# Chunk ends of the first pass in three parts, set-up transposes a block later, more of layer 1 left for the tail

## The chip, the cores and the metric

The kernel runs on one core of a Trainium2 chip. The metric is the device time of one execution in microseconds (us). The core's engines run side by side, each in its own order: PE does matrix products (and transposes, as products with the identity), DVE (VectorE) and ACT (ScalarE) do elementwise work, POOL (GpSimd) small elementwise work and part of the DMA issues, SP (SyncE) the other DMA issues. They meet at semaphores.

## The reference

Two layers over N = 4096 nodes with 512 features each; `adj` is a 0/1 matrix of 4096 x 4096.

```python
# layer 0, H = 8 heads of FH = 64
feats = einsum('nf,hfo->hno', X, W)
dense = s_self[:, :, None] + s_neigh[:, None, :]     # feats . a_self, feats . a_neigh
dense = where(dense > 0, dense, 0.2 * dense) * A
out   = einsum('hij,hjo->hio', softmax(dense), feats) + b
x     = layernorm(x + relu(out))
# layer 1, 32 graphs of 128 nodes each
a      = where(mask, query @ key.T * scale, 0.0)     # mask: same graph
scores = (a + adj + adj) * where(mask, 1.0, -1e6)
x      = layernorm(x + (softmax(scores) * mask) @ value)
```

In layer 0 a pair without an edge has the score 0 and still counts in the softmax with weight 1. So a row of layer 0 is a sum over its neighbours, plus the sum of all features, minus the neighbours' plain features, over a matching denominator.

## The kernel before, in words

The function `adjacency_streamed_path` does the work. (A general path, chosen by a flag, is not run with these inputs.) It has a set-up, four passes over the adjacency matrix and a tail.

**Order.** `tc.manual_schedule(engines={mybir.EngineType.PE})` (L455) makes PE run in program order: the order in which the Python code issues matmuls is PE's order. The orders of DVE, ACT, POOL and SP are chosen by a scheduler when the kernel is built. Tiles come from pools with a fixed number of buffers (`bufs`); an instruction that fills a tile waits until the last reader of the tile that had the buffer before is done.

**Set-up (L578 to L794).** Eight blocks k of four row tiles u (128 nodes each). A block turns the rows of x (L635), makes the features of each tile (`features`, four products that the trace records as four matmuls each for u, L715), the scores (`scores`, L644), their exponentials (`exponentials`, L658 on PE, the rest on ACT and DVE), and the rows of exponentials: `rows_of_exponentials` transposes on PE (L694), copies the result to `pu_row` on ACT (L698) and stores it to DRAM (L702). `columns_of_exponentials` transposes `pu_row` back on PE (L707) and copies it to `pu_all` on DVE (L708). `scaled_features` scales a tile on DVE and ACT (L729, L737, L738) into staging tiles `gst` and `fst` (two buffers each) and stores them to DRAM (POOL, L750), from where the passes read them as `g_s` and `f_s`. At the end PE makes the sum of all features (L785, `S_col`).

**A pass (`main_pass`, L1264).** There are four passes r, each for two heads. A pass has four chunks c of 1024 rows i; a chunk goes over 32 tiles j of 128 neighbours, in cycles of eight tiles (pass 3: four). For a cycle SP loads `f_s` and `g_s`, and from pass 1 on the adjacency tiles `at`. DVE makes `q` (L1311), the weights before the neighbour's own factor, and ACT (some on DVE, L1316) makes `mark` (L1320), which tells the branch of the leaky step. PE's part of a cycle is:

- `accf` (L1331, 32 matmuls in a cycle of eight): plain features of the neighbours;
- in pass 0 the transposes that bring the coming adjacency tiles (`bring`, L1086; ACT casts them, L1090, and POOL stores them for the later passes, L1091);
- `acc` (L1348, 128): the weighted features;
- `dens` (L1362, 32): the denominators; in pass 0 also `ae` (L1375, 16): sums of exponentials and counts of neighbours, for all heads.

In each cycle there are two places for other work, `pieces(c, group, 0)` between `accf` and `acc`, and `pieces(c, group, 1)` behind `acc`. In passes 0 to 2 `run_pieces` fills one of them: it adds a credit of 0.75 times the cycle's width (6.0 for eight tiles) and takes steps from generators until the credit is used; each `yield` says what the step before it cost. There are two queues of generators, `ends` (the ends of chunks) and `work` (weights of layer 1, L862 on; kinds of graphs); before, they are served in turns. In pass 3 the string plan `PLAN` says which generator takes a step in which place: `E` the end of a chunk, `a` and `b` a step of the first and of the second block of layer 1 of the chunk that `E` ended, `R` the layer-0 rows of its second block, and `p` (L1214) a step of what is left of the second block of the chunk before it.

**A chunk's end (`sums_to_rows`, L1125).** Right away, `ys` takes `accf` and `acc` (DVE, L1133 and L1141), and ACT copies `dens` to `dcs` and, in pass 0, `ae` to `aes` (L1143, L1146). PSUM tiles `acc`, `accf` and `dens` have one buffer each, so the next chunk's matmuls wait for these reads. The rest is the generator `pieces`, which first yields a cycle:

- in pass 0, `pz`: eight products of `aes` with `comb` (L1154); DVE makes `n0` and `z_all` of it;
- `pd`: four transposes of `dcs` (L1173); DVE makes `parts` (L1176) and from it `rd`, one over the denominators (L1186 to L1189);
- `fin`: eight transposes of `ys` in two banks (L1196), which DVE scales by `rd` into `hst` (L1197, one buffer); `hst` goes to DRAM as `hs_d` (POOL, L1209), or in pass 3, with the other passes' parts read back as `hp_l`, into the rows of layer 0 (`rows_of_layer_0`, L1121) and on to the two generators of layer 1 for this chunk.

Scratch PSUM banks for all these are handed out in turn by `misc`: two in pass 0, three later.

**Layer 1 (`layer_1`, L929 on)** takes a block of 512 rows in steps: two of transposing its rows (x1T, L935), two of zT (L955, eight matmuls each), one of scores with exponentials (L982; DVE L991, ACT L1016 on), then V, pT, V (L1027, L1056), po (L1041) with layernorm, V and po again, whose rows go to `out`. Behind the passes a last string (`run_plan("bEpppaa...")`) does what is left: the tail.

Of the kernel before, what the change touches and what calls it, by code (L numbers as in the profile page):

```python
# [19 lines left out]
P = 128  # L20
# [384 lines left out]
def adjacency_streamed_path(  # L405
# [172 lines left out]
    with tc.tile_pool(name="setup1", bufs=1, side="right") as one, tc.tile_pool(  # L578
# [174 lines left out]
        for k in range(NB):  # L753
            if k + 1 < NB:
                load_rows(k + 1)
            fbs = [features(k, 0)]
            if k == 0:
                fbs.append(features(k, 1))
                scores(0)
            else:  # L760
                exponentials(k)
            if k + 1 < NB:
                turn_rows(k + 1)
            if k == 0:
                exponentials(0)
            scaled_features(k, 0, fbs[0])
            if k:
                fbs.append(features(k, 1))
            scaled_features(k, 1, fbs[1])
            fbs.append(features(k, 2))  # L770
            scaled_features(k, 2, fbs[2])
            if k + 1 < NB:
                scores(k + 1)
            rows_of_exponentials(k)
            fbs.append(features(k, 3))
            scaled_features(k, 3, fbs[3])
            columns_of_exponentials(k)
            if k in (4, 5, 6):
                tc.keep_in_program_order(load_adjacency(0, 4 * (k - 4)))
        xsum = one.tile([P, FC], F32, name="xsum")  # L780
# [2 lines left out]
        for r in range(PR):  # L783
# [8 lines left out]
        nc.vector.scalar_tensor_tensor(  # L792
            S_col, b_col, float(N), pS, op0=OP.mult, op1=OP.add
        )  # L794

    psa = ctx.enter_context(tc.tile_pool(name="ps_acc_f", bufs=1, space=PSUM))
    dens = psa.tile([P, HB], F32, name="dens")
# [6 lines left out]
    def kind_of_scores(lp):  # L804
        ok = lp.tile([P, 5], F32, name="ok")
        ext = lp.tile([P, 5], F32, name="ext")
        for i, (v, op) in enumerate(
            ((p_all, OP.max), (d_all, OP.max), (p_all, OP.min), (d_all, OP.min))
        ):
            rows = lp.tile([P, NT], F32, name="rows")  # L810
            nc.vector.tensor_reduce(rows, v, AX.X, op)
            nc.vector.tensor_reduce(ext[:, i : i + 1], rows, AX.X, op)
        nc.vector.tensor_reduce(ext[:, 4:5], n0, AX.X, OP.min)
        nc.vector.tensor_scalar(ok[:, 0:2], ext[:, 0:2], P_MAX, None, op0=OP.is_le)
        nc.vector.tensor_scalar(ok[:, 2:4], ext[:, 2:4], 1.0 / P_MAX, None, op0=OP.is_ge)
        nc.vector.tensor_scalar(ok[:, 4:5], ext[:, 4:5], N / 2.0, None, op0=OP.is_ge)
        nc.vector.tensor_reduce(okp, ok, AX.X, OP.add)

    def kind_of_graphs(lp):

# [304 lines left out]
    def sums_to_rows(r, c, acc, accf, ae, u_row, later_by):  # L1125

        its = slice(c * CT, (c + 1) * CT)
        pair = slice(2 * r, 2 * r + 2)  # L1130

        y = evp.tile([P, C], F32, name="ys")
        nc.vector.scalar_tensor_tensor(  # L1133
            y,
            accf.rearrange("p s n -> p (s n)"),
            S_col[:, r : r + 1],
            u_row,
            op0=OP.add,
            op1=OP.mult,
        )  # L1140
        nc.vector.tensor_add(y, y, acc.rearrange("p s n -> p (s n)"))  # L1141
        dcs = evp.tile([P, HB], F32, name="dcs")
        nc.scalar.copy(dcs, dens)  # L1143
        if r == 0:
            aes = pools["aes"].tile([P, HB], F32, name="aes")
            nc.scalar.copy(aes, ae)  # L1146

        def pieces():
            if r < PR - 1:
                yield later_by  # L1150
            if r == 0:
                pz = misc([P, CT, H + 1])
                for t in range(CT):
                    nc.tensor.matmul(  # L1154
                        pz[:, t, :],
                        aes[:, ts(t % 4, P)],
                        comb[:, t // 4, :],
                        start=(t == 0),
                        stop=True,
                        skip_group_check=True,  # L1160
                    )
                nc.vector.tensor_scalar(
                    n0[:, its], pz[:, :, H], -1.0, float(N), op0=OP.mult, op1=OP.add
                )
                z = z_all[:, its, :]
                nc.vector.tensor_tensor(
                    z, u_all[:, its, :], n0[:, its, None].to_broadcast([P, CT, H]), OP.mult
                )
                nc.vector.tensor_tensor(z, pz[:, :, :H], z, OP.add)
                yield 1.5  # L1170
            pd = misc([P, 4, P])
            for t in range(4):
                nc.tensor.transpose(pd[:, t, :], dcs[:, ts(t, P)], ident)  # L1173
            parts = small.tile([P, 2, 4, 2, 2], F32, name="parts")
            for s in range(2):
                nc.vector.tensor_reduce(  # L1176
                    parts[:, s],
                    pd[:, :, 64 * s : 64 * s + 64]
                    .rearrange("p t (h m) -> p t h m", h=2)[:, :, :, :6]
                    .rearrange("p t h (k i) -> p t h k i", k=2),  # L1180
                    AX.X,
                    OP.add,
                )
            parts = parts.rearrange("p s t h k -> p (s t) h k")
            rd = small.tile([P, CT, 2], F32, name="rd2")
            nc.vector.tensor_tensor(rd, parts[:, :, :, 1], p_all[:, its, pair], OP.mult)  # L1186
            nc.vector.tensor_tensor(rd, parts[:, :, :, 0], rd, OP.add)
            nc.vector.tensor_tensor(rd, rd, z_all[:, its, pair], OP.add)
            nc.vector.reciprocal(rd, rd)  # L1189
            if r == 0:  # L1190
                yield 0.6
            hst = hp_.tile([P, CT, FP], F32, name="hst")
            for t4 in range(0, CT, 4):
                fin = misc([P, 4, FP])
                for t in range(4):
                    nc.tensor.transpose(fin[:, t, :], y[:, ts(t4 + t, P)], ident)  # L1196
                nc.vector.tensor_tensor(  # L1197
                    hst[:, t4 : t4 + 4, :].rearrange("p t (h o) -> p t h o", h=2),
                    fin.rearrange("p t (h o) -> p t h o", h=2),
                    rd[:, t4 : t4 + 4, :, None].to_broadcast([P, 4, 2, FH]),  # L1200
                    OP.mult,
                )
                if t4 == 0:
                    if r == PR - 1:
                        first = rows_of_layer_0(2 * c, hst, pools["lp"])
                    if r == 0:
                        yield 0.6
            if r < PR - 1:
                nc.gpsimd.dma_start(  # L1209
                    hs_d[ts(c, C), ts(r, FP)].rearrange("(t p) n -> p t n", p=P), hst  # L1210
                )
            else:
                args = pools["lp"], pools["lp1"], pools["lp2"]
                plan["p"] = plan["b"]  # L1214
                plan["a"] = layer_1(2 * c, first, *args)

                def second():
                    rows = rows_of_layer_0(2 * c + 1, hst, pools["lp"])
                    plan["b"] = layer_1(2 * c + 1, rows, *args)
                    yield  # L1220

                plan["R"] = second()
            yield 1.8

        return pieces()
# [4 lines left out]

    PLAN = ("Ep", ""), ("pp", ""), ("p", "a"), ("Ra", "a"), ("a", "b"), ("ba", "b"), ("ab", ""), (
        "aaba",
        "",
    )
    plan = {"p": None, "b": None}

    def run_plan(todo):
        for k in todo:  # L1240
# [3 lines left out]
            if k == "E":  # L1244
                ends.pop(0)

    state = {"credit": 0.0, "worked": True}

    def run_pieces(budget):

        state["credit"] += budget
        while state["credit"] > 0.0 and (work or ends):
            queue = ends if ends and (state["worked"] or not work) else work
            state["worked"] = queue is work
            try:
                state["credit"] -= next(queue[0])
            except StopIteration:
# [6 lines left out]
    def main_pass(r, ae=None, wide=4):  # L1264

        for c in range(NCH):
# [9 lines left out]
                )  # L1276
            def pieces(c, group, place):
                if r == PR - 1 and c:
                    run_plan(PLAN[group][place])
                elif place == (r == 0):  # L1280
                    run_pieces(0.75 * wide)

# [115 lines left out]
    at2 = wide_passes.enter_context(tc.tile_pool(name="more_at", bufs=MORE))  # L1398
    q2 = wide_passes.enter_context(tc.tile_pool(name="more_q", bufs=2))
    more["at"], more["q"] = (at2, MORE), (q2, 2)  # L1400
    with tc.tile_pool(name="ps_ae", bufs=1, space=PSUM) as psx, tc.tile_pool(
        name="aes", bufs=1
    ) as pools["aes"]:
        ae = psx.tile([P, HB], F32, name="ae")
        nc.vector.memset(ae, 0.0)
        banks.append(psx)
        main_pass(0, ae, wide=8)
        run_pieces(999.0)
        banks.remove(psx)
    first_pass.close()  # L1410
    banks.extend([ctx.enter_context(tc.tile_pool(name="ps_misc2", bufs=2, space=PSUM))] * 2)
# [2 lines left out]
    with tc.tile_pool(name="wl1", bufs=1, side="right") as wp:  # L1414
        work.append(weights_of_layer_1(keep, wp))
        work.append(kind_of_graphs(wp))
        kind_of_scores(wp)
        main_pass(1, wide=8)
        for gen in work:
            for _ in gen:  # L1420
# [5 lines left out]
    with tc.tile_pool(name="lp", bufs=2) as lp, tc.tile_pool(  # L1426
# [2 lines left out]
        pools.update(lp=lp, lp1=lp1, lp2=lp2)  # L1429
        main_pass(3)  # L1430
        plan["K"] = kind_of_inputs(lp1)
        run_plan("bEpppaaRaaKKbbababaababbbb")


@with_exitstack
# [50 lines left out]
```

## Time and profile before

| | us |
|---|---|
| median of four runs (2119.07 to 2122.23) | 2121.45 |
| the profiled execution's own time | 2116.37 |
| its span in the profile | 2114.0 |
| PE busy (97% of the span) | 2059.8 |
| DVE busy (79%) | 1660.2 |
| ACT busy (73%) | 1540.2 |
| a cycle of eight tiles in pass 0 / one with a chunk's end | 25.79 / 32.15 |
| a cycle of eight tiles in pass 1 | 23.13 |

The profile is one execution, which took some 5 us less than the median. Its span runs from the first to the last recorded instruction. Busy time is the sum of an engine's instructions; idle time of PE is put down to what released the instruction that ended it. A row `PE ps_m L1154 <- ACT aes L1146` is time in which PE's instruction at line 1154, writing tile `ps_m`, waited for ACT's instruction at line 1146. Ends of matmuls are modelled, so a longer duration of the same group of matmuls means that it was issued more slowly.

### The profile page before, as it was taken

How to read it: one execution, taken by the hardware profiler on the slowest of the kernel's cores; microseconds unless marked ns; L12 is line 12 of the kernel's file. 1: busy time of each engine (PE TensorE's matmuls, PEld its weight loads, DVE VectorE, ACT ScalarE, POOL GpSimd, SP SyncE). 2: the span in 40 equal slices, each digit the busy share in tenths (PEclk: the TensorE clock that was granted, in tenths of full speed). 3: DMA queues.
4: the chain of work that ended last, by engine and by line, in shares of the span. 5: the costliest groups of instructions: out<-in, count | busy, mean ns of one | idle time of the engine just before them, and what ended most of it. 6: DMA issues, size and time to landing. Idle time of an engine off the chain costs nothing. (4 is left out here: it accounts for less than half of the span.)

```text
span 2114.0 us, 38159 instructions
## 1 busy us (share of the span) xinstructions
PE 2059.8 (97%) x15012; PEld 1019.2 (48%) x15012; DVE 1660.2 (79%) x2032; ACT 1540.2 (73%) x1820; POOL 247.0 (12%) x391
## 2 busy tenths in 40 slices
PE   8999999999999999999999999999999999999987
PEld 4445554555554444545444544444454444445443
DVE  5547887878779978799999999999975884886554
ACT  3327997978859888798899889998875576567420
POOL 2333222222200000000000000000300110110110
PEclk9999999999999999999999999999999999999999
DMA  7889999999988998799999999989974673675211
GB/s 244 265 219 232 288 283 273 275 269 261 291 285 311 325 324 298 265 315 328 334 326 348 307 328 342 327 286 363 308 240 143 228 252 133 229 263 165 70 48 42
DMA packets 207882, 551.29 MB, mean 261 GB/s; under 512 B 25292, under 2 KB 66252, under 8 KB 207692
## 3 DMA queue, kind: packets, MB, share of 16 engines
q1 hardware_dynamic: 140748, 425.79, 58.2%
q0 software_dynamic: 62784, 121.91, 23.0%
q8 instruction: 120, 1.97, 0.4%
q10 hardware_dynamic: 4160, 1.05, 0.2%
q14 instruction: 70, 0.57, 0.1%
HBM read 491.79 MB, written 107.22 MB: 283 GB/s over the span
## 5 line engine op out<-in xcount | busy, mean ns | idle before, releaser
L1311 DVE SCALAR_TENSOR_TENSOR q<-p_row,d_all,at 128x1024 f32<-128x1024 f32 x1024 | 1241.3, 1279 | 177.2 <-PE acc L1348 141.0
L1320 ACT ACTIVATE mark<-q,nb_all 128x1024 fp8e4<-128x1024 f32 x896 | 996.9, 1145 | 205.3 <-DVE q L1311 179.0
L1348 PE MATMUL acc<-q,g_s 128*32 128x512 f32 x8192 | 903.5, 593 | 3.7 <-DVE q L1311 3.2
L1348 PEld LDWEIGHTS acc<-q,g_s 128*32 128x32 f32 x8192 | 264.1, 110 | 598.6 <-issue 536.5
L1331 PE MATMUL accf<-at,f_s 128*128 128x512 f32 x2048 | 493.2, 397 | 1.9 <-issue 1.9
L1331 PEld LDWEIGHTS accf<-at,f_s 128*128 128x128 f32 x2048 | 380.2, 189 | 110.5 <-issue 29.1
L1105 ACT ACTIVATE ck<-ck,neg_half_f 128x1024 f32<-128x1024 f32 x128 | 145.9, 1140 | 19.8 <-DMA ck<-in_adj_dram 19.6
L1106 ACT ACTIVATE ck<-ck,neg_quarter 128x1024 f32<-128x1024 f32 x128 | 146.3, 1143 | 1.8
L1090 ACT CAST at<-ps_m 128x1024 fp32r<-128x1024 fp8e4 x128 | 120.2, 1025 | 14.5 <-issue 10.3
L1362 PE MATMUL dens<-mark,e_b 128*6 128x512 fp8e4 x2048 | 126.3, 384 | 0.0
L715 PE MATMUL ps_set<-w_sb_f,xT_f 128*128 128x512 f32 x256 | 118.8, 614 | 0.0
L1027 PE MATMUL ps_m<-wvT,x1T 128*128 128x512 f32 x256 | 114.3, 594 | 4.1 <-DVE parts L1176 4.0
L955 PE MATMUL ps_m<-x1T,M_sb 128*128 128x512 f32 x256 | 113.0, 595 | 1.2 <-ACT x1T L936 1.2
L1209 POOL DMA_DIRECT2D hs_d<-hst x12 | 10.8, 897 | 843.4 <-DVE hst L1197 744.3
L1316 DVE TENSOR_SCALAR mark<-q,d_all 128x1024 fp8e4<-128x1024 f32 x128 | 95.9, 749 | 5.1 <-DVE q L1311 0.5
L1362 PEld LDWEIGHTS <-e_b 128*6 128x6 bf16 x2048 | 54.3, 87 | 83.4 <-issue 41.9
L1091 POOL DMA_DIRECT2D at_d<-at x128 | 69.1, 540 | 167.3 <-ACT at L1090 91.7
L737 ACT ACTIVATE fst<-fb 128x512 fp32r<-128x512 f32 x32 | 20.3, 636 | 87.3 <-DMA f_d<-fst 53.1
L955 PEld LDWEIGHTS ps_m<-x1T,M_sb 128*128 128x128 f32 x256 | 48.0, 190 | 62.8 <-issue 59.1
L1027 PEld LDWEIGHTS ps_m<-wvT,x1T 128*128 128x128 f32 x256 | 47.7, 190 | 60.1 <-issue 57.7
L715 PEld LDWEIGHTS ps_set<-w_sb_f,xT_f 128*128 128x128 f32 x256 | 49.8, 202 | 51.4 <-issue 51.0
L1035 DVE TENSOR_TENSOR v_t<-ps_m,bv_row 128x512 f32<-128x512 f32 x32 | 21.8, 681 | 63.0 <-PE ps_m L1027 63.0
(172 smaller groups left out, 1142.0 us busy)
## 6 DMA issues: line engine op xcount, KB each, us to landing
at<-at_d SPq DMA_DIRECT2D x384, 512.0 KB, 6.0
ck<-in_adj_dram SPq DMA_DIRECT2D x128, 512.0 KB, 5.2
f_s<-f_d SPq DMA_DIRECT2D x128, 512.0 KB, 7.5
at_d<-at POOLq DMA_DIRECT2D x128, 512.0 KB, 14.7
g_s<-g_d SPq DMA_DIRECT2D x128, 256.0 KB, 5.5
f_d<-fst POOLq DMA_DIRECT2D x32, 512.0 KB, 6.1
p_row<-pu_d SPq DMA_DIRECT2D x32, 512.0 KB, 6.6
a_b<-in_adj_dram POOLq DMA_DIRECT2D x32, 512.0 KB, 17.0
```

The costliest lines, as they stand in the source:

```text
L715: nc.tensor.matmul(pf, tile_j(xTs[k][:, c].rearrange("p u n -> p (u n)"), u), w_sb[:, c, :], start=(c == 0), stop=(c == FC - 1),)
L955: nc.tensor.matmul(pz, L1["M"][:, f, ts(c, P)], x1T[:, f, :], start=(f == 0), stop=(f == FC - 1),)
L1027: nc.tensor.matmul(pv, x1T[:, f, ts(u, P)], L1["wvT"][:, f, :], start=(f == 0), stop=(f == FC - 1),)
L1090: nc.scalar.copy(at, both[:, :, k])
L1105: tc.keep_in_program_order(nc.scalar.activation(ck, ck, AF.Square, bias=neg_half))
L1106: nc.scalar.activation(ck, ck, AF.Abs, bias=neg_quarter, accum_out=binp[:, k : k + 1])
L1311: nc.vector.scalar_tensor_tensor(q, p_row[h], d_j, ats[r, c, j].bitcast(F32), op0=OP.max, op1=OP.mult)
L1316: nc.vector.tensor_scalar(mark, q, d_j, None, op0=OP.is_gt, saturate=False)
L1320: nc.scalar.activation(mark, q, AF.Sigmoid, bias=nb_all[:, j, hh : hh + 1], scale=BIG, saturate=False,)
L1331: nc.tensor.matmul(accf[:, s, :], f_s[j // 4][:, j % 4, w, :], ats[r, c, j][:, ts(s, HB)], start=(j == 0 and w == 0), stop=(j == NT - 1 an ...
L1348: nc.tensor.matmul(acc[o : o + 32, s, :], g_s[j // 4][:, j % 4, h, o % FH : o % FH + 32], qs[j, h][:, ts(s, HB)], start=(j == 0), stop=(j ...
L1362: nc.tensor.matmul(dens[lo : lo + 6, :], e_b[:, j, 2 * r + h, :], marks[j, h][:, ts(s, HB)], start=(j == 0), stop=(j == NT - 1),)
```

## The change

It has these parts:

1. **Set-up.** `columns_of_exponentials(k)` (L707) is issued a block later, behind `features(k + 1, 1)`; the last one behind `S_col`.
2. **Ends of pass 0.** The generator yields a whole cycle (`later_by`) after `pz` and after `pd`, and nothing between the two halves of `fin`. So `pz`, `pd` and `fin` run in the second, third and fourth cycle of the next chunk; before, they ran one after the other in the second.
3. **The last end of pass 0.** `run_pieces(999.0)` behind pass 0 is gone; this end runs in the second to fourth cycle of pass 1, and three scratch banks serve it there.
4. **`aes`** has no buffer of its own; it takes the one buffer of `hst`.
5. **Queues.** `run_pieces` serves `ends` first, then `work`; layer 1's weights come about a chunk later in pass 1, and `kind_of_scores` becomes a generator in `work`.
6. **Pass 3.** The first group of a chunk is `bE` for `Ep`: the other block's V, pT, V comes ahead of `pd` and `fin`. The last chunk has a plan of its own for its last two groups, without two steps of block `b` (one zT step and the scores), and these run in the tail, around the last chunk's end.

```diff
             scaled_features(k, 0, fbs[0])
             if k:
                 fbs.append(features(k, 1))
+                columns_of_exponentials(k - 1)
             scaled_features(k, 1, fbs[1])
...
             fbs.append(features(k, 3))
             scaled_features(k, 3, fbs[3])
-            columns_of_exponentials(k)
...
             S_col, b_col, float(N), pS, op0=OP.mult, op1=OP.add
         )
+        columns_of_exponentials(NB - 1)
...
         nc.vector.tensor_reduce(okp, ok, AX.X, OP.add)
+        yield 0.0
...
         if r == 0:
-            aes = pools["aes"].tile([P, HB], F32, name="aes")
+            aes = hp_.tile([P, CT, FP], F32, name="hst")
+            aes = aes.rearrange("p t n -> p (t n)")[:, :HB]
             nc.scalar.copy(aes, ae)
...
                 nc.vector.tensor_tensor(z, pz[:, :, :H], z, OP.add)
-                yield 1.5
+                yield later_by
             pd = misc([P, 4, P])
...
             nc.vector.reciprocal(rd, rd)
             if r == 0:
-                yield 0.6
+                yield later_by
             hst = hp_.tile([P, CT, FP], F32, name="hst")
...
                         first = rows_of_layer_0(2 * c, hst, pools["lp"])
-                    if r == 0:
-                        yield 0.6
...
-                plan["p"] = plan["b"]
                 plan["a"] = layer_1(2 * c, first, *args)
...
-    PLAN = ("Ep", ""), ("pp", ""), ("p", "a"), ("Ra", "a"), ("a", "b"), ("ba", "b"), ("ab", ""), (
-        "aaba",
-        "",
-    )
-    plan = {"p": None, "b": None}
+    PLAN = [("bE", ""), ("bb", ""), ("b", "a"), ("Ra", "a"), ("a", "b"), ("ba", "b")]
+    PLANS = PLAN + [("ab", ""), ("aaba", "")], PLAN + [("a", ""), ("aa", "a")]
+    plan = {"b": None}
...
-            queue = ends if ends and (state["worked"] or not work) else work
-            state["worked"] = queue is work
+            queue = ends or work
...
                 if r == PR - 1 and c:
-                    run_plan(PLAN[group][place])
+                    run_plan(PLANS[c == NCH - 1][group][place])
...
-    with tc.tile_pool(name="ps_ae", bufs=1, space=PSUM) as psx, tc.tile_pool(
-        name="aes", bufs=1
-    ) as pools["aes"]:
+    with tc.tile_pool(name="ps_ae", bufs=1, space=PSUM) as psx:
...
         main_pass(0, ae, wide=8)
-        run_pieces(999.0)
         banks.remove(psx)
...
-        kind_of_scores(wp)
+        work.append(kind_of_scores(wp))
...
-        run_plan("bEpppaaRaaKKbbababaababbbb")
+        run_plan("bEbbbbbaaRaaKKbbababaababbbb")
```

More of the change, by code (lines that the diff above doesn't have):

```diff
@@ L1245, in run_plan @@
                 ends.pop(0)
-    state = {"credit": 0.0, "worked": True}
+    state = {"credit": 0.0}
     def run_pieces(budget):
```

## The prediction

> **What bounds the kernel now.** I read the busy shares first, then the waits of TensorE (PE), then PE's timeline at each place that the diff touches.
>
> ```profile
> PE 2059.8 (97%) x15012; PEld 1019.2 (48%) x15012; DVE 1660.2 (79%) x2032; ACT 1540.2 (73%) x1820; POOL 247.0 (12%) x391
> ```
>
> PE is the bound, and its order is written by hand. The span is 2114.0 us, so about 54 us are idle; some 12 of these are the output chain at the very end. No PE instruction is removed, so a gain can only be idle time, or matmuls that ran slowly after idle time. In the view of PE's waits (total us, times, longest) I look for those that the edits touch:
>
> ```profile
> PE ps_set L707 <- ACT pu_row L698: 6.4, 3, 3.5
> PE ps_m L1027 <- DVE parts L1176: 4.0, 2, 2.0
> PE ps_m L1154 <- ACT aes L1146: 3.4, 1, 3.4
> PE ps_m L1196 <- DVE rd L1186: 2.3, 3, 0.8
> ```
>
> L707 is the set-up transpose, L1154/L1196 the first pass's chunk ends, L1027 the last pass's chunk boundaries. The timelines (start us, duration us, instruction, idle before) show what each wait drags along. Set-up, PE then ScalarE (ACT):
>
> ```profile
> 66.96 3.60 PE L715 MATMUL ps_set<-w_sb_f,xT_f 128*128 128x512 f32 x8
> 73.06 0.41 PE L707 MATMUL ps_set<-ident_f,pu_row 16*128 16x16 f32 x4 [2.50 <-ACT pu_row L698]
> 73.41 5.41 PE L715 MATMUL ps_set<-w_sb_f,xT_f 128*128 128x512 f32 x8
> ```
> ```profile
> 71.40 0.63 ACT L737 ACTIVATE fst<-fb 128x512 fp32r<-128x512 f32 x1 [7.80 <-DMA f_d<-fst]
> 72.40 0.60 ACT L698 COPY pu_row<-ps_set 16x512 f32<-16x512 f32 x1
> ```
>
> The eight L715 after the wait take 5.41 us instead of 3.60. Behind the wait is a store: ACT sat 7.80 us until a staging tile (two buffers) had been written out, and pu_row was queued behind it.
>
> A chunk end inside pass 0, and the last one, at the pass's edge:
>
> ```profile
> 332.94 1.95 PE L1154 MATMUL ps_m<-comb,aes 128*128 128x9 f32 x16
> 334.75 0.64 PE L1173 MATMUL ps_m<-ident_f,dcs 128*128 128x128 f32 x4
> 336.16 1.71 PE L1196 MATMUL ps_m<-ident_f,ys 128*128 128x128 f32 x8 [0.78 <-DVE rd L1186]
> 337.81 2.88 PE L1362 MATMUL dens<-mark,e_b 128*6 128x512 fp8e4 x32
> ```
> ```profile
> 615.25 2.64 PE L1154 MATMUL ps_m<-comb,aes 128*128 128x9 f32 x16 [3.40 <-ACT aes L1146]
> 617.74 1.09 PE L1173 MATMUL ps_m<-ident_f,dcs 128*128 128x128 f32 x4
> 619.36 1.94 PE L1196 MATMUL ps_m<-ident_f,ys 128*128 128x128 f32 x8 [0.52 <-DVE parts L1176]
> 620.95 8.59 PE L1331 MATMUL accf<-at,f_s 128*128 128x512 f32 x32
> ```
>
> And a boundary of pass 3, where PE goes to V (L1027) while VectorE (DVE) still owes it the bank:
>
> ```profile
> 1659.03 3.67 PE L1027 MATMUL ps_m<-wvT,x1T 128*128 128x512 f32 x8 [2.00 <-DVE parts L1176]
> 1672.57 3.11 PE L1348 MATMUL acc<-q,g_s 128*32 128x512 f32 x16 [0.71 <-DVE q L1311]
> ```
>
> **What the Trainium skill says.** "TensorE: Matmul & The Clock Gate", section "What's actually happening": after an idle window of about 3.4 us the array's clock falls to half. The trace agrees in kind (5.41 against 3.60 us above), and already after 2.50 us idle. Same page, "Architectural detail": ScalarE and VectorE take their queues strictly in order; that is pu_row behind fst. "DMA: Bandwidth & Descriptors", section "Anatomy of one DMA": a transfer has about 2.0 us fixed plus bytes over 436 GB/s, an estimated 3.2 us for the 512 KB hs_d store; the trace shows 3.8 to 4.9 us in pass 0, which I use. "ScalarE: Activation LUTs", section "What ACT_TABLE_LOAD costs": 1283 ns a table; here L1320's load takes 1.28 us.
>
> **The change, part by part.** The profiled execution took 2116.37 us (span 2114.0, 2.4 around it), 5.1 below the median 2121.45. I sum against the former and carry the gain over to the latter.
>
> *Set-up.* L707 moves behind eight L715 of the same block and eight of the next, some 14 us of PE work with the transposes between, so a pu_row that is 3.5 us late is in time. Waits 6.4 us, and two slow groups of eight (5.41 and 5.40, 1.8 over each, 3.6) make 10.0 at most. But the stores remain: where ACT waits 7.80 and 8.83 us for them, all 16 DMA engines are at a share of 1.0, and near the end ACT waits 4.42 and 1.86 more, just ahead of pass 0's first casts, for which PE already waits 2.0. A faster PE meets these sooner. Floor 2 (nearly all given back at the start of pass 0), ceiling 10; I take **7.0**. The last four L707 fall behind S_col: 0.4, only moved.
>
> *Pass-0 ends.* A cycle of eight tiles takes 25.79 us, one with an end 32.15 (three times): +6.35. PE's own work of that is 1.8 + 0.45 + 0.95 = 3.2; the other 3.15 are the wait on rd (0.78), one on the hst bank (0.2 to 0.4), a dens of 2.88 against 1.91, and small gaps. With a whole cycle between parts, rd is ready long before. New: fin now comes in the chunk's last cycle, so on DVE hst (2 x 0.65) goes ahead of ys (L1133), for which the next chunk's accf waits; an estimated 0.3 to 0.5 comes back. The dens slowness may partly stay. Each end 0 to 3.2, taken 2.0; three make **6.0**.
>
> In the same edit aes loses its own buffer for the hst slot. The copy into it now waits until the preceding hs_d store (issued on POOL some 4 us after that cycle's acc, now behind the cycle's at_d stores, landing 3.8 to 4.9 us later, so acc + 8 to 9, up to 11) has landed. In ACT's order the copy comes about acc + 10.4. I cost it at nothing, hidden by ACT's casts and marks before it. Without that cover ACT stands, behind it stand the sigmoid marks (1.145 each) and casts, then dens, then PE.
>
> *Edge of pass 0.* The 9.1 us from ae's end (611.84) to accf (620.95) and 1.0 of slow accf (8.59 against 7.58) go: 10.1. The end's 3.2 us of PE work comes back in cycles two to four of pass 1. The at tiles of j 4 to 7 are issued from 611.22 and need about 6 us; without the nine idle us PE may stand for them and a cooled clock, estimated 2.2 (1 to 6). Gain 0.9 to 5.9, taken **4.7**. DVE is at 22 of 23.13 us a cycle here, and gets the end's small work on top; layer 1's weights give way, a chunk later, and still fit in pass 1. Taken 0 (-2 to +2).
>
> *Boundaries of pass 3.* Two chunks lose about 4.1 us (2.00, 0.71 and an acc of 9.1 for 7.0) and 2.9 (2.01 and an acc of 7.9 for 7.0). Now V pT V stands ahead of pd and fin, so parts has 7.9 us more. But fin's second bank needs v_t of the second V, which on DVE stands behind the sums that wait for the loads hp_l (1.85 and 0.64 of wait in before): 2.3 and 1.0 come back, with the acc slowness gone. **3.5** (0 to 5).
>
> *Tail.* Two steps of the last chunk's second block, zT8 (6.87) and sc16 (3.57), move behind the last dens: the loop, full there, is 10.4 shorter. The tail gets the 10.4 and may hide it in its idle 6.0 (0.42 + 1.64 + 2.95 + 0.21 + 0.73) between the last dens (1998.46) and zT16 (2026.79). But the order is now zT8, pd, fin, sc16, V, pT, and pT needs the exponentials of these scores. On DVE they stand behind fin's sums and statistics, which in before were done 9.5 us after fin. Scores out at fin + 10.4, POOL's subtractions, a table load 1.28 and exponentials: pT at fin + 13.9, with only sc16 and V (7.2) to cover it, so a new wait of 6 to 7 us. Then 0.6 + 3.6 + 1.1 + 7.4 + 2.0 + 2.2 and about 1.2 of small waits: zT16 at fin + 32. Fin ends at dens + 8.3, so zT16 at dens + 40.3, against 28.3: 12.0 later for 10.4 saved. **-1.5** (-4 to +4).
>
> Sum: 7.0 + 6.0 + 4.7 + 3.5 - 1.5 = 19.7. The profile would show 2096.7, the median **2101.8**.
>
> **Rivals.** *Given back in part:* the set-up gains 2 because the stores set its pace, the tail loses 4, the edge gains 1; with ends 6 and boundaries 3.5 that is 8.5 less, so 2112.9. For it: DMA shares of 1.0; against: the waits on the stores leave ACT some 3 us of slack a block (e_all waits 24.7 us in seven blocks for PE). *The waits only change name:* PE gets no idle back but 2 to 3 us; 2119. For it: three of the four waits are on engines that stay as loaded. Against: rd, parts and pu_row are late by order, not by load. *The change is slower:* ACT's aes copy waits for the hs_d store. Three of four chunk ends have such a store before them (chunk 0's has none). From a landing after acc + 13 on, past ACT's slack of up to 2.5 us, each us is one of PE's; stores of 12 us, the worst f_d landing (11.9), would cost 16 - 13 = 3 us of wait, some 3 of slow matmuls and the marks' late restart, 10 an end at most: 3 x 10 - 19.7 = 10 slower, 2132. Against: hs_d itself never landed that late in pass 0. *It doesn't do what it says* is ruled out: the built order of PE shows each part in its new place.
>
> **Numbers.** Forecast 0.50 (own range 2094 to 2108), given back 0.29, waits renamed 0.10, slower 0.11. No change means within 0.2%, 4.2 us, which is about what a measurement of this kernel tells from none: 2117.2 to 2125.7. Faster 0.79, same 0.10, slower 0.11. The low end takes ends at 3, set-up at 10 and the tail at 0, which is 27: 2094. The high end holds the given-back case and half the renamed one: 2119.
>
> **What would show it.** Right: no L707 wait and no L715 group of eight above 4 us in set-up; cycles of pass 0 with a part at 25.79 + 0.5 to 2; no wait of 3.40 at pass 1's start; V ahead of fin without its 2.0; a wait on pT4 of about 6 us after the last dens. Wrong: a new PE wait at pass 0's first casts (set-up given back), on marks after a chunk end behind aes (slower), on at or accf in pass 1's first cycle, or a tail longer by more than 14 us.

## The result and the profile after

The changed kernel takes 2116.48 us (median of 34 runs), the kernel before 2119.71 us on the same chip (median of 55). The ratio is 0.9986, with a 95% interval of 0.9978 to 0.9993: about 3 us faster, where 19.7 were forecast. The profiled execution took 2114.31 us with a span of 2112.2; before it was 2116.37 and 2114.0.

The table cuts both spans at the same points of the program: the starts of `accf` groups on PE, read from PE's timeline. A gain is positive; the sum is the difference of the spans.

| stretch | before, us | after, us | gain | forecast |
|---|---|---|---|---|
| start to pass 0's first `accf` | 180.05 | 174.62 | 5.4 | 7.0 |
| five cycles of pass 0 (to chunk 1's second) | 130.60 | 131.20 | -0.6 | 0 |
| on to the last chunk's second cycle (ends of chunks 0 and 1) | 219.10 | 215.71 | 3.4 | 4.0 |
| on to the second cycle of pass 1's second chunk (end of chunk 2, edge, last end) | 209.88 | 205.38 | 4.5 | 6.7 |
| rest of pass 1 and one cycle | 305.19 | 307.79 | -2.6 | 0 |
| rest of pass 2, and pass 3 up to its third chunk | 606.98 | 607.36 | -0.4 | 0 |
| two chunk boundaries of pass 3, last chunk, tail | 462.20 | 470.14 | -7.9 | 2.0 |

So the first five rows brought 10.1 of 17.7, and the end of the kernel lost 7.9. (The -0.6 is in the first two cycles of pass 0, whose `accf` take 9.14 and 7.87 us for 8.84 and 7.58.) The page of after has PE busier, 98% for 97%: the same 15012 instructions took 3.6 us longer. PE's waits (us in total, times, longest) have changed their names:

```profile
PE 2063.4 (98%) x15012; PEld 1017.6 (48%) x15012; DVE 1660.3 (79%) x2032; ACT 1535.3 (73%) x1818; POOL 249.2 (12%) x391
```
```profile
PE ps_m L1029 <- DVE y_f L1045: 6.8, 2, 3.4
PE ps_m L1058 <- ACT ns L1009: 4.1, 1, 4.1
PE ps_m L1088 <- DVE pu_all L708: 3.8, 1, 3.8
PE accf L1330 <- DMA at<-at_d: 3.0, 1, 3.0
```

All four waits of before that the prediction aimed at (6.4, 4.0, 3.4 and 2.3 us) are gone. These four are new. In code lines, L1029 is V (L1027 before), L1058 pT, L1088 the transposes of `bring`, L1330 `accf`. PE's timeline (start, duration, idle before) at the four places, in the order of the kernel; the end of set-up:

```profile
165.44 0.61 PE L707 MATMUL ps_set<-ident_f,pu_row 16*128 16x16 f32 x4
165.97 1.03 PE L1088 MATMUL ps_m<-ident_b,a_b 128*128 128x128 bf16 x8
170.79 1.96 PE L1088 MATMUL ps_m<-ident_b,a_b 128*128 128x128 bf16 x16 [3.78 <-DVE pu_all L708]
...
601.87 3.92 PE L1330 MATMUL accf<-at,f_s 128*128 128x512 f32 x16 [0.73 <-PE ae L1374]
608.80 6.74 PE L1330 MATMUL accf<-at,f_s 128*128 128x512 f32 x16 [3.01 <-DMA at<-at_d]
...
1668.52 3.60 PE L1029 MATMUL ps_m<-wvT,x1T 128*128 128x512 f32 x8
1675.53 5.40 PE L1029 MATMUL ps_m<-wvT,x1T 128*128 128x512 f32 x8 [3.41 <-DVE y_f L1045]
...
2005.15 1.63 PE L1058 MATMUL ps_m<-ident_f,ns 128*128 128x128 f32 x4 [4.12 <-ACT ns L1009]
2006.58 5.76 PE L1029 MATMUL ps_m<-wvT,x1T 128*128 128x512 f32 x8
```

Each wait costs more than itself: behind 3.41 us idle a V takes 5.40 for 3.60 (6.58 at the other boundary), behind 3.01 the half of `accf` takes 6.74 for 3.9, behind 4.12 a pT and a V take 1.63 and 5.76 for 0.60 and 3.60. The trace has the reason: over these slow groups the mean granted TensorE clock is 0.55 to 0.69 of full speed (0.69 from 1675.5 to 1681.0 us), and 1.00 just ahead of that wait.

What PE waits for at the boundary is in DVE's timeline, between PE's two V (and, below it, the normalisation's place in the kernel before):

```profile
1668.11 1.91 DVE L530 TENSOR_SCALAR x1b<-x1b,mv_f,rstd_f 128x512 f32<-128x512 f32 x4 [1.26 <-POOL rstd_f L528]
1669.94 4.86 DVE L1310 SCALAR_TENSOR_TENSOR q<-p_row,d_all,at 128x1024 f32<-128x1024 f32 x4
1674.73 1.40 DVE L1045 SCALAR_TENSOR_TENSOR y_f<-ps_m,rd_f,x1b 128x512 f32<-128x512 f32 x2
```
```profile
1670.32 1.00 DVE L530 TENSOR_SCALAR x1b<-x1b,mv_f,rstd_f 128x512 f32<-128x512 f32 x2 [0.92 <-POOL rstd_f L528]
```

The `po` matmuls of this cycle were done at 1668.7. Their banks are read by `y_f`, but DVE, in its order, first normalises the rows that the chunk's end made and makes four `q`. Counted from the chunk's first `accf`, the normalisation begins after 26.0 us, where it was 18.5 before. The second V needs one of those banks.

### The profile page after: what moved, and what is told of

It reads as the page before. It is cut to its first block, busy times and chain, and to the rows that moved or that the text cites. A ratio compares the mean times of both kernels' runs of the same rounds, so it can differ in the third digit from the quotient of the medians.

```text
span 2112.2 us, 38133 instructions
## 1 busy us (share of the span) xinstructions
PE 2063.4 (98%) x15012; PEld 1017.6 (48%) x15012; DVE 1660.3 (79%) x2032; ACT 1535.3 (73%) x1818; POOL 249.2 (12%) x391
## 5 line engine op out<-in xcount | busy, mean ns | idle before, releaser
L1330 PE MATMUL accf<-at,f_s 128*128 128x512 f32 x2048 | 496.4, 398 | 3.8 <-DMA at<-at_d 3.0
L1330 PEld LDWEIGHTS accf<-at,f_s 128*128 128x128 f32 x2048 | 380.9, 189 | 115.2 <-issue 26.3
L1029 PE MATMUL ps_m<-wvT,x1T 128*128 128x512 f32 x256 | 121.1, 622 | 6.8 <-DVE y_f L1045 6.8
L715 PE MATMUL ps_set<-w_sb_f,xT_f 128*128 128x512 f32 x256 | 116.4, 603 | 0.0
L1093 POOL DMA_DIRECT2D at_d<-at x128 | 69.0, 539 | 176.7 <-ACT at L1092 105.9
L1029 PEld LDWEIGHTS ps_m<-wvT,x1T 128*128 128x128 f32 x256 | 50.3, 200 | 66.7 <-issue 56.4
L715 PEld LDWEIGHTS ps_set<-w_sb_f,xT_f 128*128 128x128 f32 x256 | 49.0, 199 | 49.7 <-issue 49.4
```

What stands on the lines that cost most here:

```text
L715: nc.tensor.matmul(pf, tile_j(xTs[k][:, c].rearrange("p u n -> p (u n)"), u), w_sb[:, c, :], start=(c == 0), stop=(c == FC - 1),)
L1029: nc.tensor.matmul(pv, x1T[:, f, ts(u, P)], L1["wvT"][:, f, :], start=(f == 0), stop=(f == FC - 1),)
L1330: nc.tensor.matmul(accf[:, s, :], f_s[j // 4][:, j % 4, w, :], ats[r, c, j][:, ts(s, HB)], start=(j == 0 and w == 0), stop=(j == NT - 1 an ...
```

## The experiments

All are edits to the changed kernel. Ratios are to the kernel before on the same chip; the changed kernel's is 0.9986 [0.9978, 0.9993]. One execution of one kernel strays by some us, so an experiment is read from both its ratio and the stretch of its trace that the edit touches.

**Pass 3's boundary, V behind the end again.**

```diff
-    PLAN = [("bE", ""), ("bb", ""), ("b", "a"), ("Ra", "a"), ("a", "b"), ("ba", "b")]
+    PLAN = [("Eb", ""), ("bb", ""), ("b", "a"), ("Ra", "a"), ("a", "b"), ("ba", "b")]
```

> Edit to the changed kernel: pass 3's first group is Eb in place of bE, so that pd and fin come ahead of V, pT, V again; all else stays. Theory A (V first delays the end's chain on DVE, so that the y_f of the next cycle come late and the second V of that cycle finds no bank): the two waits of 3.4 us and the slow V behind them (5.40 and 6.58 for 3.60) vanish, the two of 2.0 us on parts come back; boundaries as in the kernel before, about 7 us less than the changed kernel: 2109 to 2110. Rival B (the lost time at the boundaries lies in something else, such as later loads): the y_f waits stay, time as the changed kernel, 2116.

Measured: 2107.34 us, ratio 0.9943 [0.9925, 0.9962]. The waits on `y_f` are gone from pass 3, and the old one is back:

```profile
PE ps_m L1029 <- DVE parts L1181: 4.0, 2, 2.0
```

The stretch with the first of the two boundaries falls from 176.4 to 173.8 us (174.0 before the change), that with the second from 143.8 to 140.1: 6.3 less. By the medians it is some 9. Over the ten traces with the boundary as in the changed kernel the two stretches take 177.0 and 143.8 on average, which makes it 6.9. A holds: V first costs more than the waits that it takes away.

**V first, but `po` and V of the next group behind `acc`.**

```diff
-    PLAN = [("bE", ""), ("bb", ""), ("b", "a"), ("Ra", "a"), ("a", "b"), ("ba", "b")]
+    PLAN = [("bE", ""), ("", "bb"), ("b", "a"), ("Ra", "a"), ("a", "b"), ("ba", "b")]
```

> Edit to the changed kernel: V first stays, but po and the two V of the next group move from between accf and acc to behind acc (7 us later on PE). Theory A (y_f only comes late because DVE takes the normalisation and four q ahead of it; nothing is short): both y_f waits and the slow V vanish, 5.2 + 6.4 = 11.6 us less, about 2105. Rival B (DVE as a whole is behind here, so the wait goes to the next thing it owes, q or v_t): a gain of 0 to 3, 2114 to 2116.

Measured: 2114.24 us, 0.9976 [0.9968, 0.9984]. The `y_f` waits vanish, but PE then stands for `q`, 2.5 us at each of the two boundaries:

```profile
1671.74 8.24 PE L1347 MATMUL acc<-q,g_s 128*32 128x512 f32 x48 [2.46 <-DVE q L1310]
```

B holds: behind a boundary with V first, DVE is behind as a whole. It is not only that one instruction stands in a wrong place; putting it later moves the wait to the next thing that DVE owes. In the changed kernel DVE had stood 3.30 us for a load of `hp_l` in that stretch, with the sums of the second V and `parts` queued behind it; with the end first, in the kernel before, it was 1.85 and came behind `parts`. The load in the changed kernel's DVE:

```profile
1653.75 1.05 DVE L1123 SCALAR_TENSOR_TENSOR x1b<-hp_l,x1b 128x384 f32<-128x384 f32 x2 [3.30 <-DMA hp_l<-hs_d]
```

How much of DVE's delay is this load's and how much the later end's as such, no run separates.

**The tail, scores ahead of the chunk's end.**

```diff
-        run_plan("bEbbbbbaaRaaKKbbababaababbbb")
+        run_plan("bbEbbbbaaRaaKKbbababaababbbb")
```

> Edit to the changed kernel: in the tail the scores of the last chunk's second block come ahead of pd and fin (zT, sc, pd, fin). Theory A (pT waits 4.1 us because DVE takes the end's sums and statistics ahead of the scores, and the clock falls): the wait falls under 1.5 us, pT and V (1.63 and 5.76) run at 0.6 and 3.6, some 5 to 6 us less: 2110.5 to 2111.5. Rival B (the end's chain, 3.6 us later, is then what the first x1T waits for): the time moves there, 2115 to 2117.

Measured: 2109.86 us, 0.9965 [0.9948, 0.9982]. In the tail pT follows V with no wait, and one of 1.84 on `v_t` is new:

```profile
2003.02 0.60 PE L1058 MATMUL ps_m<-ident_f,ns 128*128 128x128 f32 x4
2003.46 3.60 PE L1029 MATMUL ps_m<-wvT,x1T 128*128 128x512 f32 x8
2006.90 1.02 PE L1043 MATMUL ps_m<-v_t,pT_f 128*128 128x512 f32 x2
2009.76 1.13 PE L1043 MATMUL ps_m<-v_t,pT_f 128*128 128x512 f32 x2 [1.84 <-DVE v_t L1037]
```

From the last chunk's last `accf` to the end it takes 143.8 us for 149.9 (148.2 to 150.5 in the other traces with the changed kernel's tail). A holds, with 6.1 for the 5 to 6 expected; the end's chain, 3.6 us later on PE, stays hidden.

**The edge of pass 0, last `ae` ahead of `acc`.** The 16 matmuls of `ae` become a function, called at one of two places.

```diff
+                last_0 = r == 0 and c == NCH - 1 and j0 + wide == NT
+                if last_0:
+                    sums_of_exponentials()
                 first = wide // 2 if r == 0 or wide == 4 else 6
...
-                if r == 0:
+                if r == 0 and not last_0:
+                    sums_of_exponentials()
```

> Edit to the changed kernel: in the last cycle of pass 0 alone the 16 ae matmuls stand between accf and acc, not behind dens, so that the adjacency tiles are free some 16 us earlier. Theory A (pass 1's first accf stands for at tiles whose loads are issued only when ae has released the buffers): the waits of 0.73 and 3.01 us and the slow accf (3.92 + 6.74 for 7.58) vanish, 6.8 less: about 2110. Rival B (those loads are late by the rate of the transfers): the wait stays, 2116.

Measured: 2111.38 us, 0.9957 [0.9942, 0.9972]. Of the edge only one short wait is left, and `accf` runs at full speed:

```profile
605.72 7.59 PE L1330 MATMUL accf<-at,f_s 128*128 128x512 f32 x32 [1.76 <-issue]
```

The same tiles were issued from 602.43 in the changed kernel and from 586.72 here. From the second cycle of pass 0's last chunk to that of pass 1 it takes 104.3 us for 109.5. That is 5.2 of the 6.8 us expected. A holds: these loads wait for `ae` to release the buffers, not for the rate of the transfers.

**Set-up transposes in their old place.**

```diff
             if k:
                 fbs.append(features(k, 1))
-                columns_of_exponentials(k - 1)
...
             scaled_features(k, 3, fbs[3])
+            columns_of_exponentials(k)
...
-        columns_of_exponentials(NB - 1)
```

> Edit to the changed kernel: the set-up transposes stand in their old place, at the end of their own block; all else stays. Theory A (the move is worth what the first accf of pass 0 shows, 174.6 against 180.1): about 5 us more than the changed kernel, 2121 to 2122. Rival B (the stores set the pace of the set-up and take it all back): as the changed kernel, 2116.

Measured: 2118.30 us, 0.9994 [0.9982, 1.0006]. The trace has pass 0's first `accf` at 179.9 us, as before (180.1). In the ten traces of kernels that share the changed set-up it comes at 174.2 to 179.0, on average 176.7. So the move is worth 3.3 us on average and 5.4 in the trace of the result; the ratio says 1.7, with an uncertainty of some 3. The time lies between A and B; the start of pass 0 is A's.

**`aes` with its own buffer.**

```diff
-            aes = hp_.tile([P, CT, FP], F32, name="hst")
-            aes = aes.rearrange("p t n -> p (t n)")[:, :HB]
+            if c < NCH - 1:
+                aes = pools["aes"].tile([P, HB], F32, name="aes")
+            else:
+                aes = hp_.tile([P, CT, FP], F32, name="hst")
+                aes = aes.rearrange("p t n -> p (t n)")[:, :HB]
```

> Edit to the changed kernel: aes has a buffer of its own again for chunks 0 to 2, and takes that of hst for the last chunk alone. Theory A (the shared buffer is hidden, as the prediction had it): no difference, 2115 to 2118. Rival B (ACT stands for the hs_d store at chunk ends, and that is the 1.3 us which the first cycle of chunk 2 takes over 25.79): 1 to 3 us less, 2113.5 to 2115.

Measured: 2114.65 us, 0.9979 [0.9970, 0.9989]. The ratio alone doesn't tell it from the changed kernel. The trace does: the two stretches of four cycles that hold the ends of chunks 0 and 1 take 106.98 and 107.01 us; with the shared buffer 108.28 and 107.43, and in other traces 106.98 to 109.51. The three traces with an own buffer for these chunks agree to 0.01 us; the nine with the shared one and the ends in three parts are 1.0 and 0.7 longer on average. The changed kernel's ACT and PE at the second end:

```profile
397.32 0.58 ACT L1151 COPY hst<-ae 128x512 f32<-128x512 f32 x1 [4.47 <-DMA hs_d<-hst]
```
```profile
411.99 0.39 PE L1361 MATMUL dens<-mark,e_b 128*6 128x512 fp8e4 x4 [0.65 <-ACT mark L1319]
```

ACT stands 4.47 us for the store of `hst`, which takes 11.4 us here, and PE meets late marks at the cycle's end. B, though small: 1.3 and 0.4 us in this trace.

**The last set-up block's transposes left in place.**

```diff
+            if k == NB - 1:
+                columns_of_exponentials(k)
             scaled_features(k, 3, fbs[3])
...
-        columns_of_exponentials(NB - 1)
```

> Edit to the changed kernel: the last block's set-up transposes stay where they were (ahead of the last tile's scaling), the other seven stay moved. Theory A (pass 0's second bank waits 3.8 us and more for pu_all because DVE takes that copy behind the last tile's scaling, which waits for stores): the wait falls to 0 to 1, 3 to 4 us less than the changed kernel, 2112.5 to 2113.5. Rival B (the stores pace everything here): the wait only changes its name, to casts or to q, 2116.

Measured: 2116.43 us, 0.9985 [0.9975, 0.9996], as the changed kernel. The wait is the same one under another name:

```profile
170.60 2.03 PE L1089 MATMUL ps_m<-ident_b,a_b 128*128 128x128 bf16 x16 [3.56 <-DVE S_col L794]
```

B holds as to the wait. That the stores are behind it is for the next run to show.

**Set-up with half of its stores.**

```diff
-                nc.gpsimd.dma_start(dst[:, k, :, ts(u, n)].rearrange("r p n -> p r n"), src)
+                nc.gpsimd.dma_start(
+                    dst[:2, k, :, ts(u, n)].rearrange("r p n -> p r n"), src[:, :2]
+                )
```

The loads of `f_s` and `g_s` read `f_d[r % 2, k]` and `g_d[r % 2, k]`.

> Edit to the changed kernel: the set-up stores only the first two passes' halves of gst and fst (12.6 MB in place of 25.2), and passes 2 and 3 read those of passes 0 and 1 again; so heads 4 to 7 are computed with the features of heads 0 to 3, with the same work on every engine. Theory A (the set-up's stores take back what the moved transposes gain): ACT's 79 us of waits for f_d fall below 25, the wait for pu_all at pass 0's first transposes (3.8 us and more) falls below 1, and pass 0's first accf comes at 168 to 171 in place of 174 to 178; 4 to 6 us less in all, 2110.5 to 2112.5. Rival B (ACT's or DVE's own work is what is late): accf stays at 174 or later, 2116.

Measured: 2111.78 us, 0.9951 [0.9933, 0.9968]. ACT's waits for the `fst` stores fall from 79.0 to 11.9 us, the wait for `pu_all` is gone, and pass 0 begins 4.7 us earlier than in the trace of the result:

```profile
163.75 0.61 PE L707 MATMUL ps_set<-ident_f,pu_row 16*128 16x16 f32 x4
164.29 2.14 PE L1090 MATMUL ps_m<-ident_b,a_b 128*128 128x128 bf16 x16
...
169.94 8.60 PE L1332 MATMUL accf<-at,f_s 128*128 128x512 f32 x32
```

A holds. With half of the stores, the set-up is 10.1 us shorter than before. The prediction's ceiling for the move was 10.0, but the kernel before was not run with half of its stores, so how much of the 10.1 is the move's is not shown. (The traced execution took 2118.67 us as a whole, 7 above the median; it is read for the set-up alone.)

**Pass 0's ends in one place again.**

```diff
-                yield later_by
+                yield 1.5
...
-                yield later_by
+                yield 0.6
```

> Edit to the changed kernel: pass 0's chunk ends run in one place again (pz, pd, fin one after the other in the second cycle of the next chunk, for the last end in the second cycle of pass 1); aes, the missing flush and all else stay. Theory A (three parts save the waits between them, 1.3 to 2.4 us an end by the two traces): 5 to 7 us more than the changed kernel, 2121.5 to 2123.5. Rival B (the gain lies in something else at these ends): as the changed kernel, 2116.

Measured: 2116.62 us, 0.9988 [0.9978, 0.9998]. The ratio says B, the trace something nearer to A: the stretches with the ends of chunks 0 and 1 take 109.56 and 109.52 us, as before the change, and are 1.3 and 2.1 longer than in the trace of the result; the next row of the table, 205.3 us, is 0.1 shorter. That row hides two things. Up to the last `ae` the three parts save 2.4 us there too (79.6 for 82.0), and at the edge of the pass they lose it again: here SP issues the `at` loads 0.6 us ahead of `ae`'s end, in the changed kernel 1.3 us behind it, and `accf` loses 2.4 us and not 6.8 (no run changes SP's order alone). So by the traces the three parts are worth some 3.4 us, which lies at the edge of what the ratios allow (the difference of the two is 0.0002, and each is uncertain by 0.0008 to 0.0010). The whole trace of this run is 2120.7 us, longer for reasons elsewhere.

**The flush behind pass 0 put back**, and then the same with an own buffer for `aes` in all chunks:

```diff
         main_pass(0, ae, wide=8)
+        run_pieces(999.0)
```

> Edit to the changed kernel: the last end of pass 0 is flushed behind the pass again; all else stays. Theory A (taking the flush away was worth next to nothing, since PE's idle time moved to the wait for at tiles): from the first accf of pass 0's last chunk to pass 1's second chunk the same within 1.5 us, 2115 to 2118. Rival B (it was worth the 4.7 of the prediction): 2120 to 2122.

> Edit to the changed kernel: the last end of pass 0 is flushed behind the pass again, as in the run before this one, but aes has its own buffer for all chunks, as in the kernel before. Theory A (the 8.4 us that the flush alone cost were mainly the wait for the shared buffer, 5.1 us behind the hs_d store, and what the clock lost by it; with an own buffer, taking the flush away is worth next to nothing): 2114 to 2117. Rival B (the flush as such costs the 4.7 of the prediction or more): 2119.5 to 2124.

Measured: 2124.87 us, 1.0019 [1.0011, 1.0028], and 2121.84 us, 1.0010 [0.9997, 1.0023]. Both are on B's side by the time, and the traces show that the reason is not B's. In the first, the stretch from the second cycle of pass 0's last chunk to that of pass 1 takes 116.8 us, 7.2 more than in the changed kernel: `pz` stands for ACT's copy of `ae`, which needs the buffer that the store of `hst` still holds:

```profile
611.65 3.59 PE L1159 MATMUL ps_m<-comb,hst 128*128 128x9 f32 x16 [5.11 <-ACT hst L1151]
```

In the second, with the own buffer, from the second cycle of pass 0's last chunk to that of pass 1, it takes 108.95 us, 0.6 less than the changed kernel: the flush itself costs nothing there, as A had it. The loss is 100 us later, at pass 1's second chunk (PE, then the same place in the kernel before):

```profile
712.48 9.73 PE L1329 MATMUL accf<-at,f_s 128*128 128x512 f32 x32 [7.86 <-issue]
```
```profile
716.52 7.59 PE L1331 MATMUL accf<-at,f_s 128*128 128x512 f32 x32 [1.95 <-issue]
```

SP issues the `f_s` of this cycle at 706.5 us in the first of the two, behind a `ck` load that itself waited for ACT. In the changed kernel they were issued at 692.0 and 695.7, and `accf` doesn't wait. The scheduler gave SP another order in each of these kernels; why it did is not settled.

**Four edits together** (end first, tail's scores first, `ae` early, own buffer):

> Edit to the changed kernel: four earlier edits together: Eb for bE, the tail's scores ahead of the chunk's end, the last ae ahead of acc, and a buffer of its own for aes in chunks 0 to 2. Theory A (four losses in four places, which add up by the stages of the traces: 6.3, 6.1, 5.5 and 1.5): 19.4 less than the changed kernel, 2096 to 2099. Rival B (they overlap, or a later stage takes some back): 2102 to 2107.

Measured: 2099.25 us, 0.9902 [0.9886, 0.9918], 17.2 less than the changed kernel, against 19.4 by the sum of stages; the spans are 2095.8 and 2112.2. A holds, 0.25 us above its numbers: the four losses lie in four places and add up. In this trace the stages give 6.4 (boundaries), 6.2 (tail), 5.5 (edge) and 1.7 (buffer), together 19.8; what is missing in the span is mainly the set-up, which ends 2.5 us later than in the trace of the result. This version is faster than both kernels.

## Why the prediction was wrong

The direction was right, and the time, 2116.5, lies inside the range; but of a gain of 19.7 us 16.5 are missing. By its own steps:

- **Boundaries of pass 3 (+3.5 forecast; about -6 found).** This is the step that failed. It priced what V first takes away (2.0 and 2.0 and their slow `acc`) and the new wait of `fin` for `v_t` (1.30 and 0.89 measured, 2.3 and 1.0 said), and stopped there. It didn't ask for whom the delayed end is late next: DVE's work for the end comes 7.5 us later, into the cycle in which `y_f` has to free PSUM banks. Each boundary lost a 3.4 us wait and 1.8 to 3.0 of slow V, together 11.6; the 7.0 of the old losses less 11.6 and less the 2.2 for `v_t` is -6.8. What is late next was asked for the edit's own cycle and not for the following one.
- **Edge of pass 0 (4.7; about 0.1, which is 4.5 of the table less 2.5 for the end of chunk 2, up to the last `ae`, and less the 1.95 of an old wait at pass 1's second chunk).** The mechanism was named, the loads of `at` behind the last `ae`, with a range of 1 to 6 us; it took 6.8 (0.73 + 3.01 idle, 3.1 of slow `accf`), where 2.2 was put in. Most of it could have been worked out: the loads are issued when `ae` ends and take 6 us, the half of `accf` that doesn't need them takes 3.9. SP's order seems to have a share too: in the one-place run, with the loads issued 1.9 us sooner against `ae`'s end, PE lost 2.4.
- **Set-up (7.0; 5.4 in this trace, 3.3 on average).** Mechanism right, the giving-back larger: ACT's waits for stores rose from 53 to 79 us, and at pass 0's first transposes 3.3 to 6.1 us came back in the ten traces. The stores are the cause, as the half-store run shows. (The moved transposes stand behind sixteen L715 of the next block, not eight; the 14 us are right.)
- **Ends of chunks 0 to 2 (6.0; some 5.9).** Right in kind, with the waits named; that the sum fits is in part luck, as two errors cancel. With an own buffer each end gains 2.6 us, not 2.0, and the buffer, costed at nothing, takes 1.3 and 0.4 of it: the `hs_d` store landed after 11.4 and 9.8 us at the first two ends in place of 3.8 to 4.9, since it now starts behind four `at_d` stores. In the one-place run, with the store back at its old place, it took 3.9 to 4.4. The duration was taken from a trace in which the store was issued at another place.
- **Pass 1 (0; -2.6 behind its first chunk, and the 1.95 us wait gone).** Of the -2.6, 0.8 is a wait of the weights' transposes for `hst`, and 1.7 are 16 matmuls of layer 1's biases that took 6.06 for 4.38. The 1.95 is an accident of SP's order.
- **Tail (-1.5; -2.1 in one pair of traces).** Right, by its own chain. The wait was 4.1 us, not 6 to 7, but the slow matmuls behind it add 3.2. The -2.1 is from the end-first run: from pass 3's third chunk on only the last chunk differs there from the kernel before, and it takes 464.3 us for 462.2.

Of the rivals, "the waits only change name" comes nearest in number: 2 to 3 us of gain, and some 3 were measured. But its reason, engines that stay as loaded, was seen only at pass 3's boundaries, where DVE is behind as a whole; the small sum is 10.1 gained less 7.9 lost. "Given back in part" (8.5 of gain) was right on the edge and, by the average, on the set-up; the boundaries, which cost most, it took at +3.5 like the forecast. "The change is slower" had its mechanism confirmed (ACT does stand for `hs_d`, 4.5 us) at a tenth of its price; the 11.9 us that it takes for the worst `f_d` landing is a `g_d` store's, the worst of `f_d` is 11.2. Of the four signs of being wrong three came: waits at pass 0's first transposes, on marks behind `aes`, and on `at` in pass 1's first cycle.

The Trainium skill ("TensorE: Matmul & The Clock Gate", section "What's actually happening") has the array's clock at half after an idle window of about 3.4 us. The traces agree in kind and add the size: waits of 3.0 to 4.1 us cost PE another 1.8 to 3.2 in slow matmuls. They differ on the threshold: behind a wait of 2.00 us the V took 5.37 us at a granted clock of 0.67 in the end-first run, and 3.67 at 1.00 in the kernel before, so the length of the wait alone doesn't tell.

## What to carry to other kernels

When work is put ahead of a chain on a shared in-order engine, follow that chain's new time to the end of the next cycle, and price the wait there together with the slow matmuls behind it. A transfer's duration holds for the place in its queue where it was measured; after a move it is a new one. Idle time of the bounding engine is only a gain if the thing that it waits for next is early too: at the edge of a pass, at the end of a set-up, it was a load or a store that had been hidden in the idle time.

## What was not expected of the hardware

The transfers of one kind on one queue differ by three times with their place: the 512 KB `hs_d` store landed after 3.8 to 4.9 us in the three ends of the kernel before, after 11.4 and 9.8 us behind four `at_d` stores in the changed one, and after 5.6 us at its third end, where no `at_d` store is in front. The same built set-up, run again in ten kernels, reached its end between 174.2 and 179.0 us, while pass 2 (from its second cycle on) took 363.35 us in most traces and at most 0.33 more in any. The load on the DMA engines doesn't tell the two apart: their mean busy share in the trace of the result is 0.87 in the set-up and 0.91 in pass 2. PE's idle time does: 13.1 us in the set-up, where PE waits for loads of `x` and for engines that wait for stores, and none in pass 2.
